# Four column strips for the softmax sums of two attention units, and their divisions one unit later

## The chip, the core and the metric

The kernel runs on one core of a Trainium2 chip. The core has five engines that work side by side[...]: TensorE (PE, matrix products into PSUM), VectorE (DVE), ScalarE (ACT), GpSimd (POOL), and SyncE (SP), which here only issues transfers. [...] The metric is the device time of one launch in microseconds, lower is better.

## The reference, cut to what matters

Four layers follow one another on an image batch x of 8 x 384 channels x 32 x 32: a convolutional attention (layer 0), a mixture of experts (layer 1), a ternary convolution (layer 2) and a deformable attention (layer 3). All arithmetic is in 32-bit floats. The change lies in layer 3, whose core is, for each image b and each of six heads of 64 channels, an ordinary softmax attention of 1024 queries over 256 sampled keys:

```python
# q: 1024 positions, k and v: 256 sampled positions, SCALE = 64 ** -0.5
attn = softmax(SCALE * q_head @ k_head.T)     # 1024 x 256
out_head = attn @ v_head                      # 1024 x 64
# then: y = proj_w @ concat(out_heads) + proj_b, added to x
```

The softmax is not applied before the product with v. The kernel forms p = exp(scores), the product of p with v, and the sums of p over the keys, and divides the product by the sums at the end. (Should a sum lie outside a safe range, a second, general path recomputes layer 3. It lies in a branch at the end of the kernel, and the data here do not enter it.)

## The kernel before, in words

**The stages.** Layer 0 fills the time up to about 1610 us. Then come the gate of layer 1, its routing, and a loop over the images that works on two images at once: layers 2 and 3 of image b (function `layers`, with `layer2` and `layer3`) and layer 1 of image b + 1 (function `layer1`, cut into pieces called units there, each of which computes one `ph` or one quarter of a `y`). `layers(b)` is a generator: it yields an idle time, and when enough is due (`UNIT`, 2.6), a piece of layer 1 is put in. In the attention, each `yield UNIT` puts in one quarter of a y: three products, L1512. For the last pair of images (6 and 7) there is no layer 1 left; layer 3 of image 6 is interleaved with layers 2 and 3 of image 7.

**The attention of layer 3** takes one image in six units: three pairs of heads (`pr`), times two halves of 512 queries (`h`). One unit goes through these steps:

- `scores` (L1862, PE): for two blocks of 128 keys, the scores of two heads, each into one bank of a 128 x 1024 PSUM tile `s`;
- `exps` (L1879, ACT): p = exp(s / 8), two tiles of 128 x 1024;
- L1924 (GpSimd): p01, the sum of the two p tiles; keys lie along the partitions, so this halves the work of the sums;
- `weigh` (L1888, PE): the product with v, `pav`, two heads in two column strips of 64;
- L1936 (DVE): a transposition of pav in blocks of 32 x 32 into `tu`, in SBUF; this frees the one PSUM bank that pav has (`vbank`, a pool of one buffer);
- `sums` (L1901, PE): p01 times a matrix of ones, `pss`, again in two column strips of 64. Each strip holds 64 equal rows: the sums of one head's 512 queries. pss is in one of three banks of the pool that `fbank` hands out, which ph and y use too;
- `divide` (DVE): pss transposed in blocks into `ts` (L1909), the reciprocal of its first columns, which now hold one query per partition (L1911), the multiplication of tu by it (L1912), and the transposition back into `att` (L1915).

**What order results.** The loop is pipelined by one: in the turn of unit u it emits p01 of u, the scores of u + 1, pav of u, the sums of u - 1, the exp of u + 1, tu of u and the division of u - 1. The six p, p, p01 groups of an image go through five SBUF buffers (`pl.flat`), and the exps wait for buffers as well as for scores. tu has two buffers, `om0` and `om1`, by turns; in the earlier part of layer 3 these tiles, and a third one, `om2`, hold sampling offsets and a mask. After unit 5, `pf` (L1991) multiplies att by proj_w, and three more tiles of layer 1 of the next image (`o`, L1421) are loaded into p buffers that have come free.

The source order is not the last word. The library that builds the program orders each engine's instructions by readiness in its own model of time, and gives buffers from a pool of free ones. The order in which they stand in the built program is fixed. One matrix product of 32-bit floats in the source makes two PE instructions in the profile.

The lines that matter most:

```python
return ps_v.tile([P, HALF], F32, tag="v", name=name)       # vbank: bufs=1
...
pss[64 * j : 64 * j + 64, :], lhsT=ones[:, :64],           # sums, L1901
...
tu = pl.one([P, NG * LS], f"om{u % 2}", f"tu_{b}_{u}")[:, :HALF]
```

Of the kernel before, what the change touches and what calls it, by code (L numbers as in the profile page):

```python
# [14 lines left out]
P = 128  # L15
KC = C // P
HALF = N // 2
# [18 lines left out]
NPAIR3, HS, LS, NG = 3, 16, 256, 3  # L36
# [19 lines left out]
def tile_kernel(ctx: ExitStack, tc: tile.TileContext, i: dict, out: bass.AP):  # L56
    nc = tc.nc
# [33 lines left out]
    ones = const.tile([P, P], F32, name="ones")  # L91
# [175 lines left out]
    with ExitStack() as pa:  # L267
# [7 lines left out]
        last = NK - 1  # L275
# [246 lines left out]
        for n, (u, kind, s) in enumerate(work):  # L522
            k, h = divmod(u, 2)
# [29 lines left out]
            if kind == "v":  # L553
                h, c = h + s, 0
# [605 lines left out]
    def fbank(name):  # L1160
        return ps_f.tile([P, HALF], F32, tag="f", name=name)
# [496 lines left out]
    def layer3(pl, b, xt, put, general):  # L1658
# [196 lines left out]
        def scores(pr, h):  # L1855

            ss = []
            for kc in range(2):
                s = big(f"s3_{b}_{pr}_{h}_{kc}")
                for j in range(2):  # L1860
                    r = slice(64 * j, 64 * j + 64)
                    nc.tensor.matmul(  # L1862
                        s[:, j * HALF : (j + 1) * HALF],
                        lhsT=kt[r, pr, kc * P : (kc + 1) * P],
                        rhs=q[r, pr, h * HALF : (h + 1) * HALF],
                        start=True, stop=True,
                    )
                ss.append(s)
            return ss

        def exps(u, ss):
            ps = []
            for kc in range(2):
                nm = f"p3_{b}_{u}_{kc}"
                if last:
                    p = third(pl, 2 * (u % 2) + kc, nm).rearrange("p a n -> p (a n)")[:, :N]
                else:
                    p = pl.flat([P, N], nm)
                nc.scalar.activation(p, ss[kc], AF.Exp, scale=0.125)  # L1879
                ps.append(p)  # L1880
            return ps
# [14 lines left out]
        if not general:  # L1896
            def sums(u, p01):

                pss = fbank(f"pss3_{b}_{u}")
                for j in range(2):  # L1900
                    nc.tensor.matmul(  # L1901
                        pss[64 * j : 64 * j + 64, :], lhsT=ones[:, :64],
                        rhs=p01[:, j * HALF : (j + 1) * HALF], start=True, stop=True,
                    )
                return pss

            def divide(pss, pr, h, u, tu):
                tss = pl.one([P, 16, 32], "ts", f"ts_{b}_{u}")
                nc.vector.transpose(tss.rearrange("p a b -> p (a b)"), pss)  # L1909
                rc = rec3[:, b * NU3 + u, :]  # L1910
                nc.vector.reciprocal(rc, tss[:, :, 0])  # L1911
                nc.vector.tensor_tensor(  # L1912
                    tu, tu, rc.unsqueeze(2).to_broadcast([P, 16, 32]), ALU.mult
                )
                nc.vector.transpose(  # L1915
                    att[:, pr, h * HALF : (h + 1) * HALF], tu.rearrange("p a b -> p (a b)")
                )


            ps, due3 = exps(0, scores(*units[0])), None  # L1920
            yield UNIT
            for u, (pr, h) in enumerate(units):
                p01 = pl.flat([P, N], f"p01_{b}_{u}")
                nc.gpsimd.tensor_tensor(p01, ps[0], ps[1], ALU.add)  # L1924
                nxt = scores(*units[u + 1]) if u + 1 < NU3 else None
                if last and nxt:
                    nxt = exps(u + 1, nxt)
                pav = weigh(pr, h, ps)
                if due3:
                    pss = sums(due3[2], due3[4])  # L1930
                if nxt:
                    ps = nxt if last else exps(u + 1, nxt)

                tu = pl.one([P, NG * LS], f"om{u % 2}", f"tu_{b}_{u}")[:, :HALF]
                tu = tu.rearrange("p (a b) -> p a b", b=32)
                nc.vector.transpose(tu.rearrange("p a b -> p (a b)"), pav)  # L1936
                if due3:
                    divide(pss, *due3[:4])
                due3 = pr, h, u, tu, p01
                yield UNIT  # L1940
                yield 0.0
            divide(sums(due3[2], due3[4]), *due3[:4])
            yield 3.0
        else:
            for pr, h in units:
                pav = vbank(f"pav3_{b}_{pr}_{h}")
                for j in range(2):
                    r = slice(64 * j, 64 * j + 64)
                    nm = f"3_{b}_{pr}_{h}_{j}"
                    s = big(f"s{nm}").rearrange("p (a k) -> p a k", a=4)  # L1950
                    for qc in range(4):
                        q0 = h * HALF + qc * P
                        nc.tensor.matmul(
                            s[:, qc, :], lhsT=q[r, pr, q0 : q0 + P], rhs=kt[r, pr, :],
                            start=True, stop=True,
                        )
                    mx = small.tile([P, 4], F32, tag="mx4", name=f"mx{nm}")
                    nc.vector.reduce_max(mx, s, AX.X, negate=True)
                    nc.vector.tensor_scalar(mx, mx, 0.125, None, ALU.mult)
                    p = pl.flat([P, 4, LS], f"p{nm}")  # L1960
                    rs = small.tile([P, 4], F32, tag="rs4", name=f"rs{nm}")
                    for qc in range(4):
                        nc.scalar.activation(
                            p[:, qc, :], s[:, qc, :], AF.Exp, bias=mx[:, qc : qc + 1],
                            scale=0.125, accum_out=rs[:, qc : qc + 1],
                        )
                    nc.vector.reciprocal(rs, rs)
                    nc.vector.tensor_tensor(
                        p, p, rs.unsqueeze(2).to_broadcast([P, 4, LS]), ALU.mult
                    )  # L1970
                    pt = pl.flat([P, 2, HALF], f"pt{nm}")
                    for kc in range(2):
                        tp = fbank(f"tp{nm}_{kc}")
                        for qc in range(4):
                            nc.tensor.transpose(
                                tp[:, qc * P : (qc + 1) * P], p[:, qc, kc * P : (kc + 1) * P], ident
                            )
                        nc.vector.tensor_copy(pt[:, kc, :], tp)
                    hd = 2 * pr + j
                    for kc in range(2):  # L1980
                        nc.tensor.matmul(
                            pav[r, :], lhsT=vt[:, kc, hd * 64 : (hd + 1) * 64], rhs=pt[:, kc, :],
                            start=(kc == 0), stop=(kc == 1),
                        )
                nc.vector.tensor_copy(att[:, pr, h * HALF : (h + 1) * HALF], pav)
# [249 lines left out]
```

## Time and profile before

| what | value |
|---|---|
| median of three runs | 3484.91 us (3483.53 to 3489.36) |
| the profiled execution, as timed | 3480.29 us |
| its span, first to last instruction | 3478.5 us |
| mean granted TensorE clock | 0.989 |
| PE busy | 3372.7 us, 97% |
| DVE busy | 1708.2 us, 49% |
| ACT busy | 1298.5 us, 37% |
| GpSimd busy | 200.1 us, 6% |
| pss products (L1901) | 192 instructions, 592 ns each in the median |
| an image period in the loop (images 2 to 3, first p01 to first p01) | 2399.76 to 2618.41 us |

Times in a timeline count from the first instruction of the profiled execution. A row of a timeline merges successive instructions of one form on one engine: the start, the time from the first start to the last end, the engine, the line, the operation, what it writes and reads, the shapes, and the number of instructions; in brackets stands the time that the engine was idle before it, and what ended that. PE instructions overlap in their ends, so the distance from one start to the next says what a step costs. In a row of a stretch, the stretch is followed by its length, the busy time of PE, PE's weight loads, DVE, ACT and GpSimd with the number of instructions, the granted clock, the transfers' share of time, and their GB/s.

### The profile page before, as it was taken

To read this page: it belongs to the slowest core of one execution; us is meant where nothing else is said; L and a number is where in the kernel's file an instruction comes from. 1 tells how busy PE (TensorE), PEld (TensorE's weight loads), DVE (VectorE), ACT (ScalarE), POOL (GpSimd) and SP (SyncE) were. 2 spreads that over 40 slices of the span, in tenths; PEclk is the share of its full clock that TensorE was granted. 3 is DMA by queue.
4 is the path that set the end of the run, shared out by engine and by line. 5 is a ranking of instruction groups with operands and counts; after the bars stand their busy time and mean duration, and the time that the engine had idled before them with its cause. 6 is when DMAs were issued, how large, how long until landed. Compare 5 with 4: busy or idle time off the path is not lost.

```text
span 3478.5 us, 44959 instructions
## 1 busy us (share of the span) xinstructions
PE 3372.7 (97%) x18599; PEld 1449.4 (42%) x18599; DVE 1708.2 (49%) x2926; ACT 1298.5 (37%) x1514; POOL 200.1 (6%) x231
## 2 busy tenths in 40 slices
PE   6999999999999999998999999999999999999888
PEld 2333434343434343443344445344453444434344
DVE  8942232323232323234266375663755637557763
ACT  5655444444444444433222322323223232331232
POOL 2100000000000000000000200102001010010022
PEclk9999999999999999999999999999999999999999
DMA  9972121212121212023600111101111011110000
GB/s 355 299 208 79 27 79 27 79 27 79 27 80 26 80 27 79 27 79 102 247 24 19 47 46 35 40 18 36 57 35 40 18 35 58 35 39 19 18 1 37
DMA packets 86260, 234.01 MB, mean 67 GB/s; under 512 B 21673, under 2 KB 21897, under 8 KB 79131
## 3 DMA queue, kind: packets, MB, share of 16 engines
q1 hardware_dynamic: 83882, 222.75, 19.8%
q10 hardware_dynamic: 1248, 4.72, 0.4%
q8 instruction: 150, 2.46, 0.3%
q0 software_dynamic: 912, 3.53, 0.3%
q14 instruction: 68, 0.55, 0.0%
HBM read 145.77 MB, written 75.59 MB: 64 GB/s over the span
## 4 chain that ended last, share of the span: by engine, by line
PE 43%; DVE 8%; DMA 1%; ACT 1%; POOL 0%; issue 0%; DVEq 0%; POOLq 0%; ACTq 0%; SPq 0%
PE y L1512 12%; PE ph L1491 10%; DVE y L1634 4%; PE pq L1684 4%; PE pw L1647 3%; PE pf L1991 3%; PE s L1862 2%; PE pav L1888 2%; DVE off L1754 1%; PE xsb L1823 1%; DVE hd L1477 1%; PE pss L1901 1%; PE pk L1837 1%; PE pv L1846 1%; PE plog L1231 1%; DMA o<-o 1%
## 5 line engine op out<-in xcount | busy, mean ns | idle before, releaser
L827 ACT ACTIVATE p<-s 128x1024 f32<-128x1024 f32 x512 | 496.3, 1021 | 365.7 <-PE s L820 365.5
L835 PE MATMUL pav<-p,vt 64*64 64x512 f32 x4096 | 494.5, 588 | 0.0
L1512 PE MATMUL y<-hd,w_sb 128*128 128x512 f32 x1080 | 487.1, 599 | 3.5 <-DVE hd L1477 3.5
L1491 PE MATMUL ph<-h,w_sb 128*128 128x512 f32 x1104 | 487.0, 595 | 1.9 <-ACT h L1440 1.8
L820 PE MATMUL s<-qk,qk 48*64 48x512 f32 x2944 | 355.0, 592 | 0.0
L1491 PEld LDWEIGHTS ph<-h,w_sb 128*128 128x128 f32 x1104 | 206.8, 190 | 262.3 <-issue 248.6
L1512 PEld LDWEIGHTS y<-hd,w_sb 128*128 128x128 f32 x1080 | 199.7, 191 | 249.0 <-issue 235.4
L835 PEld LDWEIGHTS pav<-p,vt 64*64 64x64 f32 x4096 | 167.4, 133 | 274.6 <-issue 274.4
L796 DVE COPY ta<-pav 128x512 f32<-128x512 f32 (+1 forms) x65 | 44.3, 682 | 475.3 <-PE pav L835 475.3
L1501 ACT ACTIVATE hd<-ph,b_sb 128x512 f32<-128x512 f32 x180 | 122.8, 682 | 309.9 <-PE ph L1491 309.9
L574 PE MATMUL pk<-xs,cws_sb 32*32 32x496 f32 (+3 forms) x3840 | 181.9, 605 | 38.8 <-POOL xs L402 29.4
L1754 DVE SCALAR_TENSOR_TENSOR off<-q,dw_sb,off 128x225 f32<-128x225 f32 (+3 forms) x432 | 215.8, 556 | 1.8
L1634 DVE SCALAR_TENSOR_TENSOR y<-h,tap,y 128x961 f32<-128x961 f32 (+1 forms) x168 | 203.0, 1229 | 0.5
L820 PEld LDWEIGHTS s<-qk,qk 48*64 48x64 f32 x2944 | 108.6, 133 | 212.0 <-issue 191.1
L1879 ACT ACTIVATE p<-s 128x1024 f32<-128x1024 f32 x96 | 96.2, 1023 | 165.7 <-PE s L1862 134.2
L81 DVE COPY qk<-pq 128x512 f32<-128x512 f32 x46 | 31.8, 692 | 251.8 <-PE pq L258 251.8
L1477 DVE TENSOR_TENSOR hd<-hd,cb 128x512 f32<-128x512 f32 x180 | 122.4, 685 | 37.7 <-ACT hd L1501 37.5
L574 PEld LDWEIGHTS pk<-xs,cws_sb 32*32 32x32 f32 (+1 forms) x3840 | 77.2, 111 | 141.9 <-issue 57.8
L1924 POOL TENSOR_TENSOR p<-p,p 128x1024 f32<-128x1024 f32 x48 | 113.4, 2364 | 330.0 <-ACT p L1879 329.9
L820 PE MATMUL s<-ql,ql 48*64 48x512 f32 x1024 | 128.2, 592 | 0.2 <-ACT p L827 0.2
L1991 PE MATMUL pf<-att,wp_sb 128*128 128x512 f32 x288 | 127.4, 597 | 0.0
L711 PE MATMUL pv<-wv_sb,g 128*128 128x384 f32 x384 | 127.1, 489 | 0.0
(341 smaller groups left out, 3734.5 us busy)
## 6 DMA issues: line engine op xcount, KB each, us to landing
rqk<-y SPq DMA_DIRECT2D x96, 256.0 KB
g<-rqk SPq DMA_DIRECT2D x96, 256.0 KB
xs<-in_xs_dram SPq DMA_DIRECT2D x56, 384.0 KB
g<-rv SPq DMA_DIRECT2D x48, 256.0 KB
xh<-in_x_dram SPq DMA_DIRECT2D x48, 256.0 KB
f<-in_x_dram SPq DMA_DIRECT2D x24, 512.0 KB
f<-o SPq DMA_DIRECT2D x24, 512.0 KB
o<-ot SPq DMA_DIRECT2D x42, 256.0 KB
```

Source lines behind the costliest of these rows:

```text
L574: nc.tensor.matmul(banks[r][cols[q]].rearrange("p (h w) -> p h w", w=W)[:, :, c0:c1], lhsT=cws[rs, c, 2 * h + g, x, w], rhs=src[rs, :, c0 ...
L711: nc.tensor.matmul(pv[:, :C], lhsT=acts[b][2][:, c, t * P : (t + 1) * P], rhs=w_in[2][:, c, :], start=(c == 0), stop=(c == KC - 1),)
L820: nc.tensor.matmul(s[64 * k : 64 * k + 64, j * HALF : (j + 1) * HALF], lhsT=kt[r, k0 : k0 + 64], rhs=qt[r, h * HALF : (h + 1) * HALF], sta ...
L827: nc.scalar.activation(p, s, AF.Exp, scale=scale)
L835: nc.tensor.matmul(pav[k][64 * j : 64 * j + 64, :], lhsT=vts[b % 2][r, kc, 2 * hd : 2 * hd + 2, :].rearrange("p a b -> p (a b)"), rhs=p[r, ...
L1477: nc.vector.tensor_tensor(hd, hd, state["cb"], ALU.mult)
L1491: nc.tensor.matmul(ph, lhsT=w1[:, e, c, dc * P : (dc + 1) * P], rhs=state["h1"][c], start=(c == 0), stop=(c == KC - 1),)
L1512: nc.tensor.matmul(y, lhsT=w2[:, e, dc, m * P : (m + 1) * P], rhs=state[h, k], start=(k == 0), stop=(k == NE * KC - 1),)
L1634: nc.vector.scalar_tensor_tensor(d, f, tap2[:, c, t : t + 1], d, ALU.mult, ALU.add)
L1684: nc.tensor.matmul(pq[h], lhsT=wq3[:, c, m * P : (m + 1) * P], rhs=h3[h][:, c, :], start=(c == 0), stop=(c == KC - 1),)
L1754: nc.vector.scalar_tensor_tensor(d, f, dw3[:, t : t + 1], d, ALU.mult, ALU.add)
L1991: nc.tensor.matmul(pf[:, hs], lhsT=wp3[:, pr, m * P : (m + 1) * P], rhs=att[:, pr, hs], start=(pr == 0), stop=(pr == NPAIR3 - 1),)
```

## The change

In images 0 to 6 the units 0 and 1, and the units 2 and 3, have their sums formed together. A new function `sums_of_two` puts four matrices of ones with 32 columns side by side into one pss tile (two units times two heads, four strips of 32 rows), in place of two tiles with two strips of 64. It is emitted behind the `yield UNIT` of the pair's second unit, so behind the piece of layer 1 that is put in there. One transposition into ts then serves two units. The divisions of both units (`divide_two`) are emitted in the following unit's turn. Each takes the reciprocals in four pieces of 32 partitions, since the rows of ts now hold each head once in 32 rows and rec needs them twice. tu takes three buffers by turns (`om0`, `om1`, `om2`), as tu of a pair lives longer. Units 4 and 5 keep the old form: sums of unit 4 in the turn of unit 5, sums of unit 5 behind the loop. Image 7 is unchanged.

```diff
+            def turn(rc, pr, h, tu):
+                nc.vector.tensor_tensor(
+                    tu, tu, rc.unsqueeze(2).to_broadcast([P, 16, 32]), ALU.mult
+                )
+                nc.vector.transpose(
+                    att[:, pr, h * HALF : (h + 1) * HALF], tu.rearrange("p a b -> p (a b)")
+                )
+
+            def sums_of_two(two):
+                pss = fbank(f"pss3_{b}_{two[0][2]}")
+                for k, (_, _, _, _, p01) in enumerate(two):
+                    for j in range(2):
+                        r = 64 * k + 32 * j
+                        nc.tensor.matmul(
+                            pss[r : r + 32, :], lhsT=ones[:, :32],
+                            rhs=p01[:, j * HALF : (j + 1) * HALF], start=True, stop=True,
+                        )
+                tss = pl.one([P, 16, 32], "ts", f"ts_{b}_{two[0][2]}")
+                nc.vector.transpose(tss.rearrange("p a b -> p (a b)"), pss)
+                return tss
+
+            def divide_two(two, tss):
+                for k, (pr, h, u, tu, _) in enumerate(two):
+                    rc = rec3[:, b * NU3 + u, :]
+                    for j in range(2):
+                        for e in range(2):
+                            r = 64 * j + 32 * e
+                            nc.vector.reciprocal(
+                                rc[r : r + 32], tss[64 * k + 32 * j :][:32, :, 0]
+                            )
+                    turn(rc, pr, h, tu)
+
             def divide(pss, pr, h, u, tu):
...
-                nc.vector.tensor_tensor(
-                    tu, tu, rc.unsqueeze(2).to_broadcast([P, 16, 32]), ALU.mult
-                )
-                nc.vector.transpose(
-                    att[:, pr, h * HALF : (h + 1) * HALF], tu.rearrange("p a b -> p (a b)")
-                )
-
-
-            ps, due3 = exps(0, scores(*units[0])), None
+                turn(rc, pr, h, tu)
+
+
+            ps, due3, two, ready = exps(0, scores(*units[0])), None, [], []
...
+                both = not last and u < 4 and u % 2 == 1
                 if nxt:
                     ps = nxt if last else exps(u + 1, nxt)
 
-                tu = pl.one([P, NG * LS], f"om{u % 2}", f"tu_{b}_{u}")[:, :HALF]
+                tu = pl.one([P, NG * LS], f"om{u % (2 if last else 3)}", f"tu_{b}_{u}")[:, :HALF]
                 tu = tu.rearrange("p (a b) -> p a b", b=32)
                 nc.vector.transpose(tu.rearrange("p a b -> p (a b)"), pav)
                 if due3:
                     divide(pss, *due3[:4])
-                due3 = pr, h, u, tu, p01
+                if ready:
+                    divide_two(*ready)
+                    ready = []
+                if last or u > 3:
+                    due3 = pr, h, u, tu, p01
+                else:
+                    two.append((pr, h, u, tu, p01))
                 yield UNIT
+                if both:
+                    ready, two = (two, sums_of_two(two)), []
                 yield 0.0
```

In the built program the engines' instructions differ in these sections alone. On PE the pair's sums stand behind the y quarter and ahead of the next scores, and of the two products of the sums of unit 4 one stands ahead of pav of unit 5 and one behind it. On DVE the queue around a pair runs: ts of the pair, five reciprocals, the multiplication of the first unit, one reciprocal, its transposition into att, two reciprocals, the multiplication of the second unit, its transposition, and then tu of the next unit. ACT, GpSimd and SP have the same instructions in the same order as before.

More of the change, by code (lines that the diff above doesn't have):

```diff
@@ L1905, in sums @@
                 return pss
[L1907 to L1911, printed above, removed]
+            def turn(rc, pr, h, tu):
                 nc.vector.tensor_tensor(
@@ L1917, in divide @@
                 )
-            ps, due3 = exps(0, scores(*units[0])), None
+            def sums_of_two(two):
[20 more added lines that the diff above has]
+                    turn(rc, pr, h, tu)
+            def divide(pss, pr, h, u, tu):
+                tss = pl.one([P, 16, 32], "ts", f"ts_{b}_{u}")
+                nc.vector.transpose(tss.rearrange("p a b -> p (a b)"), pss)
+                rc = rec3[:, b * NU3 + u, :]
+                nc.vector.reciprocal(rc, tss[:, :, 0])
+                turn(rc, pr, h, tu)
+            ps, due3, two, ready = exps(0, scores(*units[0])), None, [], []
             yield UNIT
```

## The prediction

> **What bounds the kernel now.** I read the busy times first, then the timeline of one image's attention (image 2; images 1 to 5 look alike), then the timelines of two places that show what the change needs.
>
> ```profile
> PE 3372.7 (97%) x18599; PEld 1449.4 (42%) x18599; DVE 1708.2 (49%) x2926; ACT 1298.5 (37%) x1514; POOL 200.1 (6%) x231
> ```
>
> TensorE (PE) is the bound: from 2399 to 2617 us, a whole image, it is busy 217.50 of 218.00 us. The timeline of units 3 to 5 (start, duration, engine, line, operation):
>
> ```profile
> 2425.45 2.35 POOL L1924 TENSOR_TENSOR p<-p,p 128x1024 f32<-128x1024 f32 x1 [5.07 <-ACT p L1879]
> ...
> 2427.05 1.31 DVE L1912 TENSOR_TENSOR tu<-tu,rec 128x512 f32<-128x512 f32 x1
> ...
> 2428.66 1.99 PE L1862 MATMUL s<-q,kt 64*128 64x512 f32 x8
> 2429.02 0.71 DVE L1518 SCALAR_TENSOR_TENSOR x<-y,yb,x 128x512 f32<-128x512 f32 x1
> ...
> 2430.58 1.94 PE L1888 MATMUL pav<-p,vt 128*64 128x512 f32 x8
> 2431.77 1.02 ACT L1879 ACTIVATE p<-s 128x1024 f32<-128x1024 f32 x1 [0.90 <-PE pav L1888]
> ...
> 2432.35 1.03 PE L1901 MATMUL pss<-p,ones 128*64 128x512 f32 x4
> 2432.57 0.72 DVE L1936 STREAM_TRANSPOSE tu<-pav 128x512 f32<-128x512 f32 x1 [1.75 <-PE pav L1888]
> ...
> 2433.43 1.94 PE L1888 MATMUL pav<-p,vt 128*64 128x512 f32 x8
> ...
> 2440.55 0.68 DVE L1912 TENSOR_TENSOR tu<-tu,rec 128x512 f32<-128x512 f32 x1
> ...
> 2442.51 9.71 PE L1991 MATMUL pf<-att,wp_sb 128*128 128x512 f32 x22
> ```
>
> Three readings. There is one bank for pav, so PE can begin pav of unit 5 (2433.43) only 0.14 us after Vector (DVE) has moved pav of unit 4 out (tu, ends 2433.29); today that tu is first in Vector's queue. A step costs its start-to-start distance: scores 1.92, pav 1.77, y 2.77, pss 0.96 us. The division (L1912) takes 0.68 us alone, but 1.31 us when it meets GpSimd's sum of p (L1924): that ends 2427.80, the division 2428.36, 0.56 later. It waits and then runs.
>
> The earlier gate product is the only work with four strips of 32 columns on 128 rows:
>
> ```profile
> 1664.48 2.78 PE L1231 MATMUL plog<-f,gate 128*32 128x512 f32 x24
> 1667.19 7.99 PE L1491 MATMUL ph<-h,w_sb 128*128 128x512 f32 x18
> ```
>
> 24 instructions in 2.71 us, 0.113 each, against 0.24 for pss in two strips: four strips do run together. Last, what an idle PE costs (image 6), and the clock in the stretch after it:
>
> ```profile
> 3365.01 1.99 PE L1862 MATMUL s<-q,kt 64*128 64x512 f32 x8
> 3369.77 3.60 PE L1888 MATMUL pav<-p,vt 128*64 128x512 f32 x8 [2.77 <-DVE tu L1936]
> ```
> ```profile
> 3371.00:3372.00 1.00, 1.00 (x4) 0.24 (x2) 1.00 (x4) 0.50 (x1) 0.00 (x0) 0.50 0.00 0
> ```
>
> After 2.77 us of idleness the granted clock is 0.50, and pav takes 3.43 us to the next start instead of 1.77. An idle 1.50 us at 3343.98 had no such effect.
>
> [...]
>
> **The change, part by part (images 0 to 5).** I count from the end of the third y part, in unit 3: Y = 2428.66 in image 2 before.
>
> *PE saved.* Before Y, three pss (2.88 us) become one pair: 8 instructions by 0.113[...], 0.96. Y comes 1.92 us earlier. The second pair replaces the pss after pav of unit 4.
>
> *Vector's order.* The built program says more than the diff: for both pairs the whole division stands ahead of the next tu, though the source has tu first. Its queue in unit 3/4 is x, statistics, ts of the pair, five reciprocals, division, reciprocal, transpose, two reciprocals, division, transpose, and then tu of unit 4, for which pav of unit 5 waits. From Y:
> - x +0.36 and statistics +1.11 as before; ts 1.75 to 2.47; the aggregation 0.25; first reciprocal 2.65.
> - Reciprocals of 32x16 are not in the trace. From 0.13 us apart (a 128x16 one to the next independent instruction, 2442.38 to 2442.51) to 0.29 (2426.76 to 2427.05, dependent). [...] I take 0.13, as they don't depend on one another: first division at 3.3, transpose 4.05 to 4.75, second division ready at 5.1.
> - GpSimd's sum of unit 5: scores now begin at 0.96, the first exp at +1.18 (2428.66 to 2429.84), the second right behind (its buffer comes free with the pair's sums instead of with pav), so it ends at 4.1, and GpSimd runs 4.2 to 6.55. The second division is caught and ends 0.55 later, 7.1; transpose to 7.84; tu to 8.50; pav of unit 5 at 8.63.
> - PE meanwhile: pair 0.96, scores 1.92, pav 1.77 to 4.65, then half of pss of unit 4, which the builder has moved up: 5.5. It stands idle 3.1 us.
>
> *The sum.* pav of unit 5 at 8.63 - 1.92 = 6.71, against 4.77 before: 1.94 late. Behind it on PE stand the rest of pss, pf, the next image's ph, pf again. I leave pss at its old length (at best 0.43 shorter), and take off 0.2 that PE waits there now: 1.75 us an image. The idle 3.1 us halves the clock[...], I take 1.5. Six images: 6 x (1.75 + 1.5) = 19.5 us.
>
> *First pair.* The same chain without the x work ends at 8.4 from the end of y in unit 1; pav of unit 3 comes at 0.96 + 1.92 + 1.77 + 2.77 + 1.92 = 9.34. Hidden by 0.9 us.
>
> *Image 6* has no y, and Vector's deformable taps (L1754) fill the queue. Division of the pair moves ahead of tu of unit 2: first division at about 3363.9, GpSimd's sum of unit 3 now from 3363.6, so caught until 3366.5; tu of unit 2 ends 3370.2 instead of 3369.7; nine taps, formerly partly in front, now follow (5 us), gelu waits for them, and the second exp of unit 4 stands behind gelu on ACT: 3377.6 instead of 3373.84. pav of unit 5 starts about 3383.1 instead of 3379.56. I take +4 (0 to 6).
>
> *At no cost.* om2 as a third tu buffer: its last reader (L1830) is done before unit 0, and the next image's use is over 100 us off; otherwise one 0.7 us wait. Two Vector transposes fewer (1.4 us) and twelve reciprocals more (1.6 at 0.13): Vector is busy 49%. The o loads (L1421): the first no longer waits for pss, the others wait for pav of unit 5 and leave about 1.5 us later; their readers on Vector are about 1 us later, and uncovered it would be the 0.87 us that PE waits for h in image 1. Behind them on SP's queue are the stores at 2448, 13 us off. The f banks see one allocation fewer a pair.
>
> Total 19.5 + 4 = 23.5 us. The profiled execution took 3480.3 (span 3478.5, 1.8 around it), so 3503.8; the median is 4.6 above it: 3508.
>
> **Rivals.** (1) Stall as above, but the clock stays: 6 x 1.75 + 4 = 14.5, 3499. [...] Against: 2.77 us sufficed. (2) The reciprocals are slow: from 0.30 us apart the first division also misses GpSimd's start at 4.2, and ends at 7.1, not the second: tu 1.7 later, and pav of unit 3 waits about 1.0: 6 x 2.7 = 16 more, 3524. (3) [...]tu ends at 7.2, the stall is 1.8 us, the clock stays, pav is 0.64 late less the 0.2; 6 x 0.44 + 4 = 6.6, 3491. (4) On the other side, faster: tu of unit 4 is in time and all of PE's saving is kept, 7 x 1.92 = 13.4, 3471. It decides at tu done by 5.5 from Y, 3 us sooner than I get[...]. (5) The strips do not run together, so nothing is saved: the gate rows speak against it; it would come on top of the stall.
>
> **How the numbers follow.** Chances: forecast 0.50, (1) 0.22, (2) 0.12, (3) 0.09, (4) 0.06, (5) 0.01. The likeliest gives 3508, its own range 3502 to 3515 ([...]image 6 from 0 to 6). For 8 in 10 I reach below (1) and to just under (2): 3493 to 3523. About 0.2%, 7 us, is what can be told from no change: faster is (4), 0.06; same is most of (3), 0.08; slower the rest, 0.86.
>
> **What would show it.** Right: pss pairs of 8 in about 1 us; a wait of pav for tu of about 3 us in images 0 to 5; clock 0.50 in some of those stretches; the division before that tu at 1.9 us or so; pf later in its image. Wrong: pav of unit 5 starting within 0.2 us of pss; reciprocals over 0.25 us apart; a scores step that waits for exp.

## The result, and the profile after

The changed kernel takes 3509.66 us (median of six runs, 3506.73 to 3511.16) against 3483.93 us (3482.68 to 3489.36) for the kernel before in the same comparison: a ratio of 1.0071, with a 95% interval of 1.0058 to 1.0084. That is 25.7 us more, and 1.7 us above the predicted 3508.

The profiled execution took 3511.1 us, its span 3509.3 us, at a mean granted clock of 0.984 instead of 0.989. The page's row of busy times of the kernel after:

```profile
PE 3381.1 (96%) x18599; PEld 1450.6 (41%) x18599; DVE 1710.5 (49%) x2996; ACT 1296.7 (37%) x1514; POOL 199.8 (6%) x231
```

PE was to do less work, and is busy 8.4 us longer. The waits, first of the kernel before and then of the kernel after (which engine and line waited for which, us in total, times, longest):

```profile
PE pav L1888 <- DVE tu L1936: 9.5, 3, 6.1
```
```profile
PE pav L1888 <- DVE tu L1964: 32.0, 9, 6.1
```

Six waits more, one in each of images 0 to 5. Image 2 shows one, in the timeline of the kernel after (weight loads and transfers left out); Y, the end of the third y part, is 2433.74:

```profile
2433.74 1.06 PE L1920 MATMUL pss<-p,ones 128*32 128x512 f32 x8
...
2435.24 0.70 DVE L1925 STREAM_TRANSPOSE ts<-pss 128x512 f32<-128x512 f32 x1
...
2436.06 1.23 DVE L1934 RECIPROCAL rec<-ts 32x16 f32<-32x16 f32 x5
...
2437.32 0.69 DVE L1908 TENSOR_TENSOR tu<-tu,rec 128x512 f32<-128x512 f32 x1
2437.98 2.35 POOL L1951 TENSOR_TENSOR p<-p,p 128x1024 f32<-128x1024 f32 x1 [4.25 <-ACT p L1879]
...
2438.42 1.02 PE L1901 MATMUL pss<-p,ones 128*64 128x512 f32 x2
...
2439.57 1.30 DVE L1908 TENSOR_TENSOR tu<-tu,rec 128x512 f32<-128x512 f32 x1
...
2441.55 0.67 DVE L1964 STREAM_TRANSPOSE tu<-pav 128x512 f32<-128x512 f32 x1
2442.37 3.50 PE L1888 MATMUL pav<-p,vt 128*64 128x512 f32 x8 [2.92 <-DVE tu L1964]
2445.68 1.90 PE L1901 MATMUL pss<-p,ones 128*64 128x512 f32 x6
...
2447.51 3.70 PE L2027 MATMUL pf<-att,wp_sb 128*128 128x512 f32 x8
```

The pair's eight products take 1.00 us to the next start (2434.74), so the four strips run together. Then Vector works through the pair's division. tu of unit 4 stands behind it in the queue: its pav ends at 2438.59, it starts at 2441.55 and ends at 2442.22, and pav of unit 5 starts 0.15 us behind it, after 2.92 us of waiting. It then needs 3.31 us to the next start, where it had needed 1.74. The same stretch by length, busy time of PE, weight loads, Vector, ACT and GpSimd, and granted clock:

```profile
2442.14:2445.55 3.41, 3.18 (x8) 1.12 (x10) 0.08 (x1) 0.00 (x0) 0.00 (x0) 0.50 0.10 10
2445.55:2448.96 3.41, 3.41 (x12) 1.16 (x9) 2.92 (x5) 0.28 (x1) 0.00 (x0) 1.00 0.78 217
```

Half clock for exactly one stretch of 3.41 us; below, such a stretch is called a dip. The trace has one dip in each of images 0 to 5, and the kernel before has none there.

**The ledger.** To see where the time goes I take the start of each image's first p01 in both traces and the difference between the two. The two profiled executions already differ by 1.66 us ahead of the first, which has nothing to do with the change. From there it grows by 2.65, 2.35, 3.49, 3.36, 3.38 and 3.96 us in images 0 to 5, 19.2 us in all, and by 9.6 us in image 6. Image 7 adds 0.3. All experiments below are read by the same two sums, "images 0 to 5" and "image 6", each against the one trace of before, because executions of one kernel spread over 4 us and more. The sums are steadier than that: three kernels with the same images 0 to 5 give +19.2, +19.4 and +19.3 there, and three with the same image 6 give +9.6, +9.7 and +9.7.

### The profile page after: what moved, and what is told of

The parts are those of the page before. It is cut to its first block, busy times and chain, and to the rows that moved or that the text cites. A ratio compares the mean times of both kernels' runs of the same rounds, so it can differ in the third digit from the quotient of the medians.

```text
span 3509.3 us, 45002 instructions
## 1 busy us (share of the span) xinstructions
PE 3381.1 (96%) x18599; PEld 1450.6 (41%) x18599; DVE 1710.5 (49%) x2996; ACT 1296.7 (37%) x1514; POOL 199.8 (6%) x231
## 3 DMA queue, kind: packets, MB, share of 16 engines
q8 instruction: 150, 2.46, 0.3%
## 4 chain that ended last, share of the span: by engine, by line
PE 43%; DVE 9%; ACT 0%; issue 0%; POOL 0%; DMA 0%; DVEq 0%; POOLq 0%; ACTq 0%
PE y L1512 12%; PE ph L1491 10%; DVE y L1634 4%; PE pq L1684 4%; PE pf L2027 4%; PE pw L1647 3%; PE pav L1888 2%; PE s L1862 2%; PE xsb L1823 1%; DVE hd L1477 1%; PE pk L1837 1%; DVE off L1754 1%; PE pv L1846 1%; PE plog L1231 1%; DVE tu L1908 1%; PE pss L1901 1%
## 5 line engine op out<-in xcount | busy, mean ns | idle before, releaser
L1888 PE MATMUL pav<-p,vt 128*64 128x512 f32 x384 | 107.1, 684 | 32.0 <-DVE tu L1964 32.0
L1684 PE MATMUL pq<-h,wq_sb 128*128 128x512 f32 x288 | 127.1, 599 | 0.0
```

The costliest lines, as they stand in the source:

```text
L1684: nc.tensor.matmul(pq[h], lhsT=wq3[:, c, m * P : (m + 1) * P], rhs=h3[h][:, c, :], start=(c == 0), stop=(c == KC - 1),)
L1888: nc.tensor.matmul(pav[64 * j : 64 * j + 64, :], lhsT=vt[:, kc, hd * 64 : (hd + 1) * 64], rhs=ps[kc][:, j * HALF : (j + 1) * HALF], start= ...
```

## The experiments

The theory: the loss of images 0 to 5 is the pair 2+3, whose division stands ahead of tu of unit 4 in Vector's queue, and the halved clock that follows PE's wait. The rivals: both pairs cost alike, the dip of the clock is no cost of its own, or the sums and reciprocals themselves cost the time.

| kernel | median us | ratio to before (95%) | images 0 to 5 | image 6 |
|---|---|---|---|---|
| after | 3509.66 | 1.0071 (1.0058 to 1.0084) | +19.2 | +9.6 |
| pair 0+1 alone | 3484.17 | 0.9999 (0.9991 to 1.0008) | -1.2 | +3.2 |
| pair 2+3 alone | 3505.73 | 1.0063 (1.0046 to 1.0080) | +22.7 | +2.8 |
| image 6 as before | 3501.23 | 1.0049 (1.0032 to 1.0066) | +19.4 | +0.2 |
| tu first | 3479.36 | 0.9985 (0.9978 to 0.9992) | -4.5 | +2.2 |
| PE kept busy | 3500.09 | 1.0044 (1.0030 to 1.0058) | +8.9 | +9.7 |
| GpSimd's sum later | 3506.53 | 1.0063 (1.0049 to 1.0077) | +15.8 | +9.7 |
| two reciprocals | 3476.28 | 0.9975 (0.9966 to 0.9985) | -7.0 | +2.6 |
| eight, cut by columns | 3478.03 | 0.9982 (0.9974 to 0.9989) | -5.2 | +2.1 |
| eight, same partitions | 3480.23 | 0.9987 (0.9980 to 0.9993) | -1.6 | +0.7 |
| PE kept busy, image 6 | 3507.54 | 1.0065 (1.0050 to 1.0080) | +19.3 | +7.1 |
| tu first, images 0 to 5 | 3476.12 | 0.9974 (0.9964 to 0.9984) | -4.2 | +0.1 |

### Each pair alone

```diff
-                both = not last and u < 4 and u % 2 == 1
+                both = not last and u == 1
...
-                if last or u > 3:
+                if last or u > 1:
```

> Units 0 and 1 alone are summed in four strips; units 2 to 5 go singly again. My theory (all of the loss in images 0 to 5 comes from the pair 2+3 standing ahead of tu of unit 4): the long wait of pav for tu and the dip of the clock are gone from images 0 to 5, and about 0.96 us an image is saved, 6 x 0.96 = 5.8; image 6 costs +3 to +5, since its first pair still pushes Vector's taps back. About 3481 to 3482 us, against 3484 before and 3510 after. The rival, that both pairs cost alike (a wait of pav of unit 3 for tu of unit 2): half of the loss stays, about 3497.

```diff
-                both = not last and u < 4 and u % 2 == 1
+                both = not last and u == 3
...
-                if last or u > 3:
+                if last or u not in (2, 3):
...
                     two.append((pr, h, u, tu, p01))
+                    due3 = None
```

> Units 2 and 3 alone are summed in four strips; units 0, 1, 4 and 5 go singly. My theory: the wait of about 2.9 us and the clock dip stay in each of images 0 to 5, and one pss less is saved there: 6 x (3.2 + 0.96) = 25 and image 6 +5 or so, about 3512 us. The rival, that both pairs cost alike: about 3497.

The pair 0+1 alone has neither the wait nor the dip in images 0 to 5; the pair 2+3 alone has the whole loss, 22.7 us. So the two pairs are not alike, and the second carries the loss: the rival falls. Two numbers were missed. The pair 0+1 was to gain 5.8 us in images 0 to 5 and gains 1.2 (3484.17 us, not 3481 to 3482). In image 2 it gains 0.72 us on PE by the start of pf (its distance from the image's first p01 falls from 37.25 to 36.53 us), of which 0.56 is lost again behind pf. The timeline of the kernel with the pair 0+1 alone, there:

```profile
2442.25 1.28 DVE L1437 SCALAR_TENSOR_TENSOR x<-o,bnsc_out,x 128x1024 f32<-128x1024 f32 x1 [0.86 <-DMA o<-o]
...
2444.44 1.12 PE L1491 MATMUL ph<-h,w_sb 128*128 128x512 f32 x2 [0.53 <-ACT h L1440]
```

Vector waits for a load of o, ACT for Vector, and the next image's ph for h, the input of layer 1 that ACT forms from x; in the kernel before, the row of that ph shows no wait of PE. By this reading, what PE gains ahead of pf is worth only what the loads of o leave of it; it stands in the trace and was not tested by itself.

The pair 2+3 alone came out 6 us below its expected 3512, and its trace shows why: it has the wait in each image, but not always the dip. PE in images 2 and 3 of this kernel:

```profile
2440.97 1.94 PE L1888 MATMUL pav<-p,vt 128*64 128x512 f32 x8 [2.92 <-DVE tu L1964]
2442.71 1.92 PE L1901 MATMUL pss<-p,ones 128*64 128x512 f32 x6
...
2662.27 3.44 PE L1888 MATMUL pav<-p,vt 128*64 128x512 f32 x8 [2.92 <-DVE tu L1964]
2665.52 1.90 PE L1901 MATMUL pss<-p,ones 128*64 128x512 f32 x6
```

The same wait of 2.92 us; pav takes 1.74 us to the next start in image 2 and 3.25 in image 3. The granted clock is 1.00 from 2440.97 to 2442.70 and 0.55 from 2662.27 to 2665.68. The clock is halved for one stretch of 3.41 us in images 1, 3 and 5, for two in image 4, and not at all in images 0 and 2. Between successive starts of pf the kernel loses 1.7 us in image 2 (no dip), 3.4, 4.2 and 4.2 in images 1, 3 and 5 (one), 5.6 in image 4 (two). So a dip costs about 2 us on top of about 1.7 us of stall. Which waits bring one is worked out in the last section.

### tu ahead of the division

```diff
+                            ins = nc.vector.reciprocal(
...
+                            tc.add_manual_dep(
+                                ins.ins, first.ins.name, mybir.DependencyInfo(
+                                    mybir.DependencyClass.NoSync, mybir.DependencyReason.DATA
+                                ), reason="tu first",
+                            )
...
-                nc.vector.transpose(tu.rearrange("p a b -> p (a b)"), pav)
+                first = nc.vector.transpose(tu.rearrange("p a b -> p (a b)"), pav)
```

The dependency is an order on Vector alone, with no semaphore: each reciprocal of `divide_two` stands behind the tu of the unit in whose turn it is emitted.

> Everything as in the change, but Vector's reciprocals of a pair stand behind the next unit's tu (an order alone, no wait added), so tu of unit 4 no longer waits for the pair's divisions. My theory: the wait of pav of unit 5 for tu and the dip of the clock vanish in images 0 to 5; the next limit is the last division, att of unit 4, for the second part of pf, so each image lies between 0.4 us below and 0.75 us above before, and image 6 between -1 and +5: about 3482 to 3493 us. The rival, that the loss is elsewhere (the sums themselves, the 12 reciprocals more, the third tu buffer): it stays near 3510.

The time falls below that of before. PE, Vector and ACT in image 2 of this kernel:

```profile
2433.06 0.72 DVE L1969 STREAM_TRANSPOSE tu<-pav 128x512 f32<-128x512 f32 x1 [2.50 <-PE pav L1888]
...
2433.70 1.25 DVE L1934 RECIPROCAL rec<-ts 32x16 f32<-32x16 f32 x5
...
2433.93 1.94 PE L1888 MATMUL pav<-p,vt 128*64 128x512 f32 x8
...
2435.66 1.92 PE L1901 MATMUL pss<-p,ones 128*64 128x512 f32 x6
...
2442.08 1.98 PE L1491 MATMUL ph<-h,w_sb 128*128 128x512 f32 x4 [0.75 <-ACT h L1440]
```

The same sums, the same reciprocals and the same three tu buffers; only tu stands first, and pav of unit 5 follows it 0.15 us after its end. Vector now idles 2.50 us ahead of tu, and PE loses nothing by it. The next limit is h again (0.75 us at ph), which takes part of the gain. That the sums, the twelve more reciprocals or the third tu buffer make the loss by themselves, wherever they stand, is ruled out.

### Is the dip of the clock a cost of its own?

```diff
                     pss = sums(due3[2], due3[4])
+                if u == NU3 - 2 and b < B - 2:
+                    spare = fbank(f"spare_{b}")
+                    for _ in range(3):
+                        nc.tensor.matmul(spare, lhsT=ident, rhs=q[:, 0, :HALF], start=True, stop=True)
```

> The change with work added in images 0 to 5: three products of 128x512 that nothing reads (six PE instructions of 0.43 us, 2.6 us), put where PE waits for tu of unit 4; the wait itself stays, and half of pss of unit 4 moves behind pav of unit 5 (0.45 us). If the dip of the clock is a cost of its own, caused by PE's idleness, it goes and takes about 1.7 us an image with it: 6 x (1.7 - 0.45) = 7.5 less than after, about 3502 us, though more work is done. If the dip costs nothing or isn't caused by idleness: 3510 to 3513.

More work, and 9.6 us less time than the kernel after. PE in image 2 of this kernel:

```profile
2434.47 2.84 PE L1961 MATMUL spare<-q,ident_sb 128*128 128x512 f32 x6
...
2438.32 1.94 PE L1888 MATMUL pav<-p,vt 128*64 128x512 f32 x8 [1.01 <-DVE tu L1968]
...
2440.06 1.91 PE L1901 MATMUL pss<-p,ones 128*64 128x512 f32 x8
...
2441.90 3.70 PE L2031 MATMUL pf<-att,wp_sb 128*128 128x512 f32 x8
```

pav starts 8.63 us after the pair's sums (2429.69), exactly as in the kernel after, so the stall is unchanged. From pav to pf it takes 3.58 us instead of the 5.14 of the kernel after (2442.37 to 2447.51). The kernel before took 3.58 too, from its pav of unit 5 at 2433.43 to this row:

```profile
2437.01 3.70 PE L1991 MATMUL pf<-att,wp_sb 128*128 128x512 f32 x8
```

So the dip costs 1.56 us up to pf in image 2, and 1.3 to 1.6 us in images 0 to 5. The trace has no half clock there: the granted clock is 1.00 from 2438.32 to 2440.06 and from 2441.90 to 2444.90. My allowance of 0.45 us for the half of pss that moves behind pav was wrong: pss behind pav takes 1.84 us with eight instructions, and 1.83 with the six that are left when two stand ahead. The two issued ahead, the half of a pss, saved nothing behind pav.

### What makes Vector late: GpSimd's sum, or the reciprocals?

First the meeting of the second division with GpSimd's sum of unit 5:

```diff
-                nc.gpsimd.tensor_tensor(p01, ps[0], ps[1], ALU.add)
+                summed = nc.gpsimd.tensor_tensor(p01, ps[0], ps[1], ALU.add)
+                if u == NU3 - 1 and b < B - 2:
+                    tc.add_manual_dep(
+                        summed.ins, divided.ins.name, mybir.DependencyInfo(
+                            mybir.DependencyClass.Sync, mybir.DependencyReason.DATA
+                        ), reason="sum behind the division",
+                    )
```

Here `divided` is the second multiplication of the pair 2+3, and the sum waits for it.

> The change, with GpSimd's sum of unit 5 in images 0 to 5 made to start behind the second division of the pair, so that this division doesn't meet it. In image 2 the division ran from 2439.57 for 1.30 us; alone it takes 0.69, so tu of unit 4 and pav of unit 5 come 0.6 us earlier: 6 x 0.6 = 3.7 less than after, 3506 us, if PE's idle 2.3 us still bring the dip; about 3497 if they don't. If the meeting with GpSimd were worth 1.3 us an image, as the third rival of the prediction had it: 3502 with the dip, 3492 without.

In image 2 of this kernel:

```profile
2437.20 0.69 DVE L1908 TENSOR_TENSOR tu<-tu,rec 128x512 f32<-128x512 f32 x1
...
2438.06 2.35 POOL L1953 TENSOR_TENSOR p<-p,p 128x1024 f32<-128x1024 f32 x1 [6.70 <-DVE tu L1908]
...
2439.38 2.73 PE L1888 MATMUL pav<-p,vt 128*64 128x512 f32 x8 [2.31 <-DVE tu L1972]
```

The division takes 0.69 us and the wait of PE falls from 2.92 to 2.31 us, as expected; the dip stays in five of the six images. So the meeting delays tu and pav by 0.6 us, not 1.3. The image gains less: by the ledger images 0 to 3 gain 0.2 to 0.5 us each and image 5 nothing, while image 4, the one without a dip, gains 2.2 of the 3.4 us in all. That the time came out at the expected 3506 is therefore luck in part.

Then the reciprocals. Three kernels follow: two of 128x16 instead of eight of 32x16; eight of 128x4; and eight of which six are 32x16, all on the same partitions. (The second and third diff show the added lines alone; the same six lines go.)

```diff
-                    for j in range(2):
-                        for e in range(2):
-                            r = 64 * j + 32 * e
-                            nc.vector.reciprocal(
-                                rc[r : r + 32], tss[64 * k + 32 * j :][:32, :, 0]
-                            )
+                    nc.vector.reciprocal(rc, tss[:, :, 0])
```

> The change with two reciprocals of 128x16 for a pair in place of eight of 32x16: it leaves out that each head's sums are put into the rows of rec twice, so the divisors are other numbers. The built order of Vector becomes two reciprocals, both divisions, both transpositions, tu. In image 2 the first division then starts about 2436.5 and the second ends at 2438.0, just ahead of GpSimd's start at 2437.98 in the kernel after; tu ends about 2440.1 instead of 2442.2 and PE idles about 0.8 us. If the number of the reciprocals and the meeting that they cause make the stall: 2.1 and the dip of 1.7 less an image, 6 x 3.8 = 23 less than after, about 3487 us. If the stall comes from the place of the divisions alone: near 3505.

```diff
+                    for c in range(0, 16, 4):
+                        nc.vector.reciprocal(rc[:, c : c + 4], tss[:, c : c + 4, 0])
```

> As the run with two reciprocals of 128x16, but each of these is cut along its columns into four of 128x4: eight instructions again, none of them on 32 partitions (it leaves the doubling of the heads' sums out as well, so the divisors are other numbers). Six of them stand ahead of the first division. If a reciprocal costs 0.25 us because it is an instruction of its own, the pair's divisions are as late as after or later, PE idles about 3 us and the clock dips: 3505 to 3510 us. If it is the 32 partitions that cost, the eight follow one another at about 0.06 us, as the two did: near that run, 3476 to 3480 us.

```diff
+                    nc.vector.reciprocal(rc, tss[:, :, 0])
+                    for i in range(3):
+                        nc.vector.reciprocal(spare3[:32, 3 * k + i], tss[:32, :, 0])
```

> Eight reciprocals for a pair again: two of 128x16 and six of 32x16, all of which read from partition 0 on and write from partition 0 on; the six go into a tile that nothing reads, and the doubling of the heads' sums is left out. If a reciprocal of 32 partitions costs 0.25 us by its size: the six stand about 0.25 apart, 1.5 us of the 1.7 that the two wide ones saved come back, PE waits for tu of unit 4 again, and the time is 3495 us or more. If it is the change of the partitions at which successive reciprocals read and write that costs[...]: the six stand 0.06 to 0.1 apart, and the time is near those of the runs with two and with eight wide reciprocals, 3476 to 3480 us.

With two reciprocals the time is 3476.28 us, 11 us below what even my theory gave. Image 2 of this kernel:

```profile
2426.57 0.31 DVE L1931 RECIPROCAL rec<-ts 128x16 f32<-128x16 f32 x2
2426.80 1.29 DVE L1908 TENSOR_TENSOR tu<-tu,rec 128x512 f32<-128x512 f32 x2
...
2428.49 2.35 POOL L1946 TENSOR_TENSOR p<-p,p 128x1024 f32<-128x1024 f32 x1 [4.25 <-ACT p L1879]
2429.23 0.68 DVE L1959 STREAM_TRANSPOSE tu<-pav 128x512 f32<-128x512 f32 x1
```

The first division starts 0.23 us behind the first reciprocal, against 1.26 us in the kernel after; both divisions are done ahead of GpSimd's sum, tu ends 5.66 us after Y (2424.25 here) instead of 8.48, and pav of unit 5 doesn't wait. Part of this is the built order, which has both divisions ahead of both transpositions here; in the kernel after, the first transposition stands between them.

Is it the number of instructions, or their 32 partitions? Vector in image 2 of the kernel with eight reciprocals cut by columns, and of the one with six on the same 32 partitions:

```profile
2427.28 0.45 DVE L1932 RECIPROCAL rec<-ts 128x4 f32<-128x4 f32 x6
2427.64 0.68 DVE L1908 TENSOR_TENSOR tu<-tu,rec 128x512 f32<-128x512 f32 x1
```
```profile
2428.35 0.41 DVE L1934 RECIPROCAL spare<-ts 32x16 f32<-32x16 f32 x3
2428.68 0.61 DVE L1909 TENSOR_TENSOR tu<-tu,rec 128x512 f32<-128x512 f32 x1
```

Eight by columns stand 0.06 us apart (six in 0.36 us to the division), and those of 32x16 that stay on the same partitions 0.11 (three in 0.33). In the kernel after five took 1.26 us, 0.25 each. So neither the count nor the 32 partitions cost: what costs is that each of the change's reciprocals starts at another partition than the one before it. In the kernel after each of the four reciprocals that change their partitions here, each 0.24 to 0.25 us long, and the division behind them, starts 0.01 to 0.03 us behind the end of the instruction before it; on the same partitions the reciprocals, each 0.18 us long, overlap and stand 0.11 us apart. The kernel with six on the same partitions also nearly keeps the order of the kernel after (division, reciprocal, transposition, reciprocals, division), so it is the clean comparison: its second division starts 4.40 us behind Y instead of 5.83, GpSimd's sum doesn't hold it, tu ends at 6.36 instead of 8.48, and PE waits 0.81 us instead of 2.92. I had expected 0.06 for the wide ones of 16 columns too, which was a misreading of a merged row; they stand 0.11 apart.

### Image 6

```diff
-                both = not last and u < 4 and u % 2 == 1
+                both = b < B - 2 and u < 4 and u % 2 == 1
...
-                if last or u > 3:
+                if b >= B - 2 or u > 3:
```

(and two buffers for tu there, as before.)

> Images 6 and 7 as before, images 0 to 5 changed. My theory, by the shifts between the two traces (image 6 lost about 9.6 us): about 3500.5 us. By the number of the prediction (image 6 costs 4): about 3505.5.

The 9.6 us are confirmed: with image 6 in its old form it costs 0.2 by the ledger, and the median, 3501.23 us, is 8.4 below that of the kernel after. What the 9.6 consist of is seen in the kernel after. Vector and GpSimd, and then PE:

```profile
3398.68 2.35 POOL L1951 TENSOR_TENSOR p<-p,p 128x1024 f32<-128x1024 f32 x1 [11.55 <-ACT p L1879]
...
3399.61 1.96 DVE L1908 TENSOR_TENSOR tu<-tu,rec 128x512 f32<-128x512 f32 x1
...
3402.03 2.34 POOL L1951 TENSOR_TENSOR p<-p,p 128x1024 f32<-128x1024 f32 x1 [1.00 <-ACT p L1879]
...
3403.14 1.77 DVE L1908 TENSOR_TENSOR tu<-tu,rec 128x512 f32<-128x512 f32 x1
```
```profile
3406.40 3.68 PE L1888 MATMUL pav<-p,vt 128*64 128x512 f32 x8 [3.73 <-DVE tu L1964]
3409.84 2.74 PE L1901 MATMUL pss<-p,ones 128*64 128x512 f32 x6
3412.51 12.71 PE L2027 MATMUL pf<-att,wp_sb 128*128 128x512 f32 x29
```

The same place in the kernel before:

```profile
3379.56 1.94 PE L1888 MATMUL pav<-p,vt 128*64 128x512 f32 x8 [0.69 <-DVE tu L1936]
...
3383.14 15.72 PE L1991 MATMUL pf<-att,wp_sb 128*128 128x512 f32 x36
```

Both divisions of the pair 2+3 meet a sum of GpSimd, 1.96 and 1.77 us instead of 0.69: 2.35 us. That this sum is lost in full is read from the trace and was not tested. And from pav to pf it takes 6.11 us, where the kernel before took 3.58, with the clock at one half (from 3404.70 to 3411.52): 2.5 us. That last part was tested, with five products that nothing reads ahead of pav of unit 5 in image 6 alone (the same edit as above, under `if u == 4 and b == B - 2`):

> The change with five products of 128x512 that nothing reads (4.3 us at full clock), put into image 6 alone, where PE waits 3.73 us for tu of unit 4. If the halved clock behind that wait is a cost of its own: from pav of unit 5 to pf 3.6 us as before, instead of 6.1, less 0.45 for the half of pss that moves behind pav, so about 2 us less after image 6, 3507 to 3508 us. If the clock isn't what makes image 6 cost more than was predicted: 6.1 us again, and 3509.7 or more.

```profile
3406.61 1.94 PE L1888 MATMUL pav<-p,vt 128*64 128x512 f32 x8 [0.95 <-DVE tu L1968]
3408.35 1.92 PE L1901 MATMUL pss<-p,ones 128*64 128x512 f32 x8
3410.20 4.13 PE L2031 MATMUL pf<-att,wp_sb 128*128 128x512 f32 x9
```

3.59 us from pav to pf. By the ledger image 6 costs 7.1 instead of 9.6. (One of the five products was placed ahead of the scores of unit 5, and pav itself comes about 1 us later in its image here, yet the image costs 2.6 us less. The medians differ by 2.1 us, 2 were expected.)

### A version that is faster than both

The pairs stay in images 0 to 5 with tu first, and images 6 and 7 keep the old form.

> Vector's reciprocals of a pair stand behind the next unit's tu, and images 6 and 7 are in the form of before: the two findings so far together. By the shifts, tu first gains 0.75 us an image in images 0 to 5 and loses 2.2 in image 6: 3484.5 - 4.5 - 0 = about 3478 to 3480, and at least 1 us below the run with tu first in all images if image 6 is where that one loses; equal to it (3479.4) if not.

3476.12 us, ratio 0.9974 (0.9964 to 0.9984): faster than the kernel before by 0.26%, and than the change by 33.5 us. It is 3.2 us below tu first in all images, of which the ledger puts 2.1 in image 6.

## Why the prediction was right

The time and the direction were right, and so was the mechanism: pav of unit 5 waits for a tu that stands behind a division caught by GpSimd's sum, and the wait halves the clock (0.50 granted for 3.41 us behind 2.92 us of waiting). Why Vector is so late was in part misread, and part of the closeness is luck. By its steps:

- **PE saved: too large by a fifth.** From the image's first full scores to Y it took 33.49 us before and takes 31.92 (2401.82 to 2433.74): 1.57 us, not 1.92. A y behind pav costs 1.87 us from pav's start, where pss behind pav had cost 1.77, so taking a pss away saves 0.86 us and not its step of 0.96; the pair costs 1.00. Of the predicted 0.96 us for the pair, 0.90 came from the gate's 0.113 us an instruction; the rest was an estimate of mine that no trace showed.
- **Vector's chain: the ends right, two errors on the way that cancel.** Counted from Y, predicted and measured: first reciprocal 2.65 and 2.32; first division 3.3 and 3.58; GpSimd's sum 4.2 to 6.55, and 4.24 to 6.59; second division ready at 5.1, and 5.83; its end 7.1 and 7.13; tu 8.50 and 8.48; pav of unit 5 8.63 and 8.63. The step that failed is "Reciprocals of 32x16 [...] I take 0.13, as they don't depend on one another": they stand 0.25 apart, and what decides is not dependence but the start partition. Two of the prediction's own signs come out accordingly: "over 0.25 us apart" was to speak against it, and they stand on that limit, 1.26 us for five; the division before tu was to take "1.9 us or so", and took 1.30. The other error is the start: "as before" gave x at 0.36, where it stands behind a transposition; in the kernel after it starts at 0.11, and the chain 0.3 us sooner than predicted.
- **Luck in that chain.** The prediction's sum let the second division be caught with reciprocals 0.13 us apart. The run with reciprocals on the same partitions, 0.11 apart and in nearly the same order, shows that this is not safe: its second division starts at 4.40, 0.16 us behind GpSimd's sum, and isn't held up; pav of unit 5 comes at 6.51, not at 8.63. So the right end rests on the reciprocals being twice as slow as was assumed. In all three runs in which they stand 0.06 to 0.11 us apart neither division is held up, and PE waits 0.8 us at most in image 2 instead of 2.9. In the order as built, the cause of the stall is the changes of the start partition, together with the sum of GpSimd that they make the second division run into.
- **PE's idle time: 3.1 us predicted, 2.92 measured.** The prediction lets PE work until 5.5, though half a pss at its step of 0.96 would end at 5.1; the half that was moved up took about as long as a whole one, until 5.7.
- **Stall: 1.75 us predicted.** pav is 2.29 us late (40.55 us from the first scores, 38.26 before) rather than 1.94, all by PE's smaller saving, and the image gives 0.36 back behind pf rather than 0.2.
- **Clock: right.** The predicted 1.5 us an image was my estimate; what the kernel before shows is 1.66 us for the pav behind 2.77 us of idleness (3.43 instead of 1.77). In the kernel after it is 1.56 in image 2 up to pf, shown by keeping PE busy, which takes 1.7 us an image off the ledger. Together 3.25 an image, measured 3.2 in the mean: 19.5 and 19.2 us.
- **First pair: right.** tu of unit 2 is done 0.98 us ahead of pav of unit 3; predicted 0.9.
- **Image 6: 4 predicted, 9.6 measured.** This is the term that was mis-sized. The prediction let pav of unit 5 come 3.5 us late and left two things out that it had priced elsewhere: GpSimd's sums on both divisions of the second pair (2.35 us) and the halved clock behind the longer wait (2.5 us). The kernel after has pav of unit 5 6.0 us late and pf 8.5. The remaining 1.2 us or so lie mostly behind pf and were not traced further.
- **The total.** The ledger gives 28.8 us, the medians 25.7; the runs of one kernel spread over 4 us and more, and the profiled execution of before, 3480.29 us, lay below all six timed runs, and that of after, 3511.1, at the upper end of its own. So part of the closeness of 3508 to 3509.66 is luck: the sum was 5 us short in image 6, and the medians lie 3 us closer together than the ledger says.

Of the rivals, "the clock stays" is refuted by one dip in each image; "slow reciprocals" would have begun at 0.30 us, and they cost 0.25; the third, in which GpSimd's sum doesn't hold up the second division, was tried, and the sum delays tu by 0.6 us (PE waits 2.31 us without it and 2.92 with it) and not 1.3, because the second division comes 0.7 us later than I had it; "the strips do not run together" is refuted by the 1.00 us. The rival on the faster side asked for tu to be done by 5.5 us after Y. With two reciprocals it is done at 5.66, pav doesn't wait, and the kernel takes 3476 us, where the rival had 3471, with PE's saving taken too large.

## What to carry to other kernels

Ask of an operation that is cut into pieces by partitions what the change of the start partition costs (0.25 us from one reciprocal to the next here, against 0.11 on the same partitions), not what the piece costs: eight small reciprocals held up a queue for 2 us where two large ones took 0.3. On a queue that releases the bound engine's only buffer, the instruction that frees it belongs first and the work that nobody awaits behind it; here that order alone turned 0.7% slower into 0.15% faster. And where a bound engine is made to wait for nearly three microseconds, price the clock that it loses in every place where it happens, the tail too: it was half of the loss in images 0 to 5 and a quarter in image 6. How long the wait is doesn't decide alone. Where it falls in the clock's grid of 3.413 us stretches does too: the same 2.92 us brought half clock in one image and not in another (next section).

## What was not expected of the hardware

The same wait brings a dip or not, by where it falls. The half-clock stretches begin on a grid of 3.413 us, all 10 in the trace of before and all 17 in that of after, so one can tell how much of a wait lies in one stretch of the grid. In images 0 to 5 of the kernel after PE is idle for 2.28, 2.23, 2.70, 2.43, 2.78 and 2.46 us of one stretch, and a dip follows each time. With the pair 2+3 alone it is 1.73, 2.28, 2.00 and 2.57 us in images 0 to 3, and a dip follows in images 1 and 3. Image 2 of that kernel is the closest case without one: its wait, 2438.05 to 2440.97, is cut by the grid at 2440.05 into 2.00 and 0.92 us. In the kernel with GpSimd's sum later, 2.2 us or more of the wait of 2.31 us lie in one stretch in five images, each with a dip; in image 4 the grid cuts it at 2880.70 into 0.81 and 1.50 us, and there is none. So in these images what counts is how the grid splits the wait; in the kernel after one stretch always holds 2.2 us or more of it. A bound can't be read from this for other places: in the kernel before a stretch with 1.65 us of idle time (from 3294.64) is followed by the full clock and one with 1.87 (from 3301.47) by half of it.

In the kernel after, the dips begin at 1998.40, 2220.27, 2442.14, 2664.00, 2885.87 and 3107.74 us, 221.87 us apart each time, which is 65 times 3.413 us. A whole number follows from the grid; that it is the same each time means that an image, 221.4 to 222.2 us from pav of unit 5 to pav of unit 5, takes nearly 65 stretches, so that the wait falls at nearly the same place of the grid in every image. The two kernels that differ from it in image 6 alone show the same spacing. In the pair 2+3 alone the wait drifts across the grid, and there are none, one or two dips in an image. Whether the loop settles at 65 stretches or only happens to be near it, no run here tried to show.

A GpSimd sum that starts within 0.2 us of Vector's division can be the one that waits: with the reciprocals on the same partitions it started at 2430.16 by the profile and took 2.99 us, while the division that began at 2430.32 took 0.62 us, as fast as one that meets nothing. With eight reciprocals cut by columns the sum began 0.2 us behind the division and took 2.66 us. Which of the two comes first is not settled by the recorded starts at that distance.
